# A preactivation block on Trainium2: x tiles on partitions 16 to 63 and 64 to 111, the first two heads' 1x1 product on quarters of TensorE, static output tiles, and the last stores over three queues

## The chip, the cores and the metric

The kernel runs on one core of one Trainium2 chip. The metric is the device time in microseconds of one execution; before the change the median of 3 runs is 3560.19 us (3558.02 to 3560.29). A core has TensorE (PE; PEld is its weight load), VectorE (DVE), ScalarE (ACT), GpSimd (POOL) and SyncE (SP), which in this kernel only issues DMAs; ACT and POOL issue some as well.[...]

## The reference

The input x is 1 x 48 x 256 x 256 in float32. Two residual layers follow each other:

```python
x = x + _L0_conv_ref(_gn(x), w_qkv, w_dw, temperature, w_proj)
x = x + _L1_conv_ref(_gn(x), Ws, Hs, Cs, 64)
# _gn: groupnorm with 16 groups of 3 channels, without scale or shift
# _L0_conv_ref:
qkv = jnp.einsum('bchw,oc->bohw', x, w_qkv)      # 1x1, 48 -> 144
qkv = dwconv3x3(qkv, w_dw)                       # depthwise
q, k, v = (heads(t) for t in jnp.split(qkv, 3, axis=1))   # 4x4 patches, padding 4, 8 heads
attn = softmax(einsum('bhcn,bhcm->bhnm', l2norm(q), l2norm(k)) * temperature)
out = fold(einsum('bhcn,bhnm->bhcm', v, attn))
out = jnp.einsum('bchw,oc->bohw', out, w_proj)
# _L1_conv_ref: sum over t of 3 terms, on windows of 64 x 64
out = jnp.einsum('bcphqw,twW,thH,tcC->bCpHqW', xb, Ws, Hs, Cs)
```

## The kernel before

The work goes through stages, here with their times in the trace from the start of the span.

Stage A (0 to 73 us): x is loaded into `xr`, a tile of 96 partitions x 128 rows x 256 columns: the upper half of the image on partitions 0 to 47 by the SP queue, the lower half on 48 to 95 by ACT's (L432). It comes in ten parts of 16, 16, 16, 16, 16, 16, 16, 8, 4 and 4 rows, and DVE runs `bn_stats` (L436) on every two rows as they come. POOL issues 35 small DMAs with the weights (L104, L108, L114). `group_stats` (L131 to L149) makes mean and rstd by small products on PE (pm, pv), `wq` (the first two heads' weights, both halves in one block diagonal of 96 x 72) and `wr` (the other six heads') are scaled with rstd (L439, L440), and products pb (L445) give the biases. Small products pk and pr (L479, one per head) prepare normalising constants; they have PSUM tiles of their own and run at 12 to 21 us.

Stage B (72 to 138): `pointwise` (L153) makes q, k and v of the first two heads. Each of its 64 products takes two rows of both halves, contracts over 96 partitions and gives 72 rows of 512 (L155; the profile lists two matmul records per product). ACT (L161) and DVE (L159) empty PSUM in turn, with the bias, into one of four rotating tiles `ot0` with 8 rows of each half. Two DMAs per tile, of 36 partitions with 8256 bytes each, go out on SP to the scratch tensor `t1` in DRAM (L493).

Stage C (138 to 287): the depthwise convolution of the first head (`depthwise_first`) reads the padded rows back from `t1` (pad), multiplies with diagonal matrices (diag) on PE, and stores qkv.

Attention (287 to 3163): for each head and block, PE multiplies keys by queries (L351), ACT takes the exponential (L588), PE multiplies with the values (L622, on quarter columns of 32), DVE adds the blocks (L636). The 1x1 product of the other six heads runs in strips (`Strip`) between these, its loads in `xs` at partitions 0 to 47 and 64 to 111, and so do the depthwise convolutions of the next head, at places that the loops write out by hand. In the last head the x tiles `xts` of the first three rounds of the next stage are loaded. `store` (L645) writes a pair of finished blocks of the last head's output to `os_` in DRAM, four DMAs a pair, all on POOL.

Stage E (3165 to 3301), the projection, in eight rounds of 16 rows of each half: SP loads `pot` (two DMAs of 48 partitions, 768 KB each, L798) and from round 3 on the x rows `pxt` (two more, L800); PE multiplies with `wp` (96 x 96, L812); DVE adds the product to x (L819) and takes `bn_stats` (L823); POOL stores the sum to `x1s` in DRAM (L828). Then SP loads windows of it as `lxq` (L785), to partitions 0 to 47 and 64 to 111, and a chain of small operations makes the second layer's statistics (L852 to L875).

The second layer (3308 to 3546) runs three products per window (L941, L965, L984) with evictions, and stores the output.

[...]a scheduler places the instructions, except in blocks whose order is written out (`manual_schedule`).

Of the kernel before, what the change touches and what calls it, by code (L numbers as in the profile page):

```python
# [17 lines left out]
C = 48  # L18
H = W = 256
HALF = H // 2  # L20
P2 = 2 * C
KS = 4
# [25 lines left out]
def conv_preact_kernel(  # L48
# [37 lines left out]
    ones = const.tile([C, 128], F32, name="ones")  # L86
# [3 lines left out]
    gm = const.tile([P2, P2], F32, name="gm")  # L90
    nc.gpsimd.dma_start(out=gm, in_=gmat)

    wq = const.tile([P2, 2 * M0], F32, name="wq")
    nc.vector.memset(wq, 0.0)
    wr = const.tile([64 + C, M1], F32, name="wr")
    wp = const.tile([P2, P2], F32, name="wp")
    nc.vector.memset(wp, 0.0)
    for s in range(2):  # L100
        r = slice(s * C, (s + 1) * C)
        for h in range(NH if s == 0 else H0):
            o = s * M0 + h * HC if h < H0 else (h - H0) * HC
            nc.gpsimd.dma_start(  # L104
                out=(wq[r] if h < H0 else wr[0:C])[:, o : o + HC].rearrange("c (z e) -> c z e", z=3),
                in_=w_qkvT.rearrange("c (z h e) -> h c z e", z=3, h=NH)[h],
            )
        nc.gpsimd.dma_start(out=wp[r, r], in_=w_projT)  # L108
# [9 lines left out]
    mean0 = const.tile([P2, 1], F32, name="mean0")  # L118
    rstd0 = const.tile([P2, 1], F32, name="rstd0")
    mean1 = const.tile([P2, 1], F32, name="mean1")  # L120
    rstd1 = const.tile([P2, 1], F32, name="rstd1")
# [8 lines left out]
    def group_stats(st, mean, rstd, pool, pspool, behind=lambda: None):  # L130

        mv = pool.tile([P2, 2], F32, name="mv")
        nc.vector.bn_aggr(mv, st.rearrange("p n s -> p (n s)"))
        pm = pspool.tile([P2, 1], F32, name="pm", tag="pstat")
# [3 lines left out]
        d = pool.tile([P2, 1], F32, name="gsd")  # L138
        nc.vector.tensor_sub(d, mv[:, 0:1], mean)
        e = pool.tile([P2, 1], F32, name="gse")  # L140
        nc.vector.scalar_tensor_tensor(e, d, d, mv[:, 1:2], ALU.mult, ALU.add)
        pv = pspool.tile([P2, 1], F32, name="pv", tag="pstat")
        nc.tensor.matmul(pv, lhsT=gm, rhs=e, start=True, stop=True)
        behind()
        f = pool.tile([P2, 1], F32, name="gsf")
        nc.vector.tensor_scalar_add(f, pv, EPS)
        g = pool.tile([P2, 1], F32, name="gsg")
# [4 lines left out]

    def pointwise(ps, dst, xs, on_vector=False):  # L153

        nc.tensor.matmul(ps[: 2 * M0], lhsT=wq, rhs=xs.rearrange("p a b -> p (a b)"), start=True, stop=True)  # L155
        src = ps[: 2 * M0].rearrange("p (a b) -> p a b", a=2)
        dst = dst[:, :, 1 : W + 1]
        if on_vector:
            nc.vector.tensor_scalar_add(dst, src, bias[: 2 * M0, 0:1])  # L159
        else:  # L160
            nc.scalar.activation(dst, src, AF.Identity, bias=bias[: 2 * M0, 0:1])  # L161
# [5 lines left out]
    class Strip:  # L167
# [5 lines left out]
        def load(self):  # L173
            self.xs = cv.tile([64 + C, SR, W], F32, name="xs", bufs=2)
            for s, rows in enumerate(both_halves(xc, SR * self.j, SR)):
                nc.sync.dma_start(out=self.xs[s * 64 : s * 64 + C], in_=rows)

        def run(self, pool):
            self.ot = ots[self.j % len(ots)]
            for i in range(0, SR, 2):  # L180
                ps = pool.tile([128, 2, 512], F32, name="big")
                for s in range(2):
                    r = slice(s * 64, s * 64 + C)
                    nc.tensor.matmul(  # L184
                        ps[:M1, s, :],
                        lhsT=wr[r],
                        rhs=self.xs[r, i : i + 2, :].rearrange("p a b -> p (a b)"),
                        start=True,
                        stop=True,
                    )  # L190
# [226 lines left out]
    with tc.tile_pool(name="xn", bufs=1) as xnp, tc.tile_pool(name="cst", bufs=1) as cst, tc.tile_pool(  # L417
        name="nps", bufs=2, space=PSUM
    ) as nps, tc.tile_pool(name="pw", bufs=4, space=PSUM) as pw:
# [5 lines left out]
        xr = xnp.tile([P2, HALF, W], F32, name="xr")  # L425
        parts = [16] * 7 + [8, 4, 4]
        st0 = cst.tile([P2, HALF * W // 512, 6], F32, name="st0")
        for i, LR in enumerate(parts):
            j = sum(parts[:i])
            for s in range(2):  # L430
                eng = nc.sync if s == 0 else nc.scalar
                eng.dma_start(  # L432
                    out=xr[s * C : (s + 1) * C, j : j + LR, :], in_=xc[:, s * HALF + j : s * HALF + j + LR, :]
                )
# [3 lines left out]

        nc.vector.tensor_scalar_mul(wq, wq, rstd0)  # L439
        nc.vector.tensor_scalar_mul(wr[0:C], wr[0:C], rstd0[0:C])  # L440
        nc.gpsimd.dma_start(out=wr[64 : 64 + C], in_=wr[0:C])
        for g, (w, k) in enumerate(((wq, P2), (wr, C))):
            m = w.shape[1]
            pb = nps.tile([128, 1], F32, name="pb0", tag="pstat")
            nc.tensor.matmul(pb[:m], lhsT=w[:k], rhs=mean0[:k], start=True, stop=True)  # L445
            nc.vector.tensor_scalar_mul(bias[:m, g : g + 1], pb[:m], -1.0)


# [16 lines left out]
        pk = nps.tile([NP1, NP1], F32, name="pk", bufs=1)  # L465
# [11 lines left out]
        pr = nps.tile([NP1, NH + 1], F32, name="pr", bufs=1)  # L477
        for i in range(NH + 1):
            nc.tensor.matmul(pr[:, i : i + 1], lhsT=row[:, i, :], rhs=ones[0:1, 0:1], start=True, stop=True)  # L479
# [4 lines left out]
        OR = 8  # L484
        for y in range(0, HALF, OR):
            ot = xnp.tile([2 * M0, OR, W + 2], F32, name="ot0", bufs=4)
            nc.gpsimd.memset(ot[:, :, 0:1], 0.0)
            nc.gpsimd.memset(ot[:, :, W + 1 : W + 2], 0.0)
            for i in range(0, OR, 2):
                ps = pw.tile([128, 512], F32, name="pw")  # L490
                pointwise(ps, ot[:, i : i + 2, :], xr[:, y + i : y + i + 2, :], on_vector=(i // 2 % 2 == 1))
            for s, rows in enumerate(both_halves(t1[0], y, OR, base=1)):
                nc.sync.dma_start(out=rows, in_=ot[s * M0 : (s + 1) * M0])  # L493
# [581 lines left out]
```

## Time and profile before

| | us |
|---|---|
| median of 3 runs | 3560.19 (3558.02 to 3560.29) |
| the profiled execution | 3547.51 |
| its span | 3545.7, at a granted clock of 0.979 |
| end of the statistics in stage A (last `bn_stats`) | 67.95 |
| first store of stage B issued, last one landed | 81.14, 137.9 |
| first depthwise product | 147.07 |
| last addition of attention | 3162.75 |
| first issue of pot, first product with it | 3165.48, 3178.16 |
| end of the projection's additions | 3300.76 |
| first product of the second layer | 3307.8 |

A line of the profile's groups gives the source line, the engine, the operation, the tiles written and read with partitions and elements, the count, then the busy time, the mean of one in ns, and the idle time of the engine just before with what ended it. A row of the stretches gives start and end, the length, the busy time of each engine in it, the granted clock of TensorE, the share of the DMA engines that was busy, and GB/s. A row of the timeline gives start, length and the instructions that follow each other. Busy matmuls can lie beside each other, so mean times count can be above the busy time.

### The profile page before, as it was taken

What the parts mean: (1) busy time and instruction counts of PE and PEld (TensorE: products, weight loads), DVE (VectorE), ACT (ScalarE), POOL (GpSimd) and SP (SyncE); (2) the same over time, 40 slices, a digit from 0 to 9 for tenths busy, and PEclk for the clock granted to TensorE, in tenths of its full rate; (3) what the DMA queues carried; (4) which work ended last, traced back from release to release, by engine and by line L of the source; (5) the groups of instructions that cost most, each with busy time, mean ns of one, the idle gap of its engine ahead of it and who ended that gap; (6) DMA issues with size and microseconds to landing.
All of it is one profiled execution on the core that took longest, in us unless ns stands there. A gap on an engine that the chain in (4) does not pass through costs nothing. (4 is left out here: it accounts for less than half of the span.)

```text
span 3545.7 us, 63152 instructions
## 1 busy us (share of the span) xinstructions
PE 3339.1 (94%) x25836; PEld 1859.1 (52%) x25836; DVE 1990.7 (56%) x2983; ACT 1900.0 (54%) x2890; POOL 562.6 (16%) x648
## 2 busy tenths in 40 slices
PE   2878999999999999999999999999999999985898
PEld 1334455555555555555555555555555555531576
DVE  5463675168726872687268727862786222238543
ACT  0245677557645664666467646764676444420343
POOL 2030112012201220122012211221122100000123
PEclk9998999999999999999999999999999999997999
DMA  7455666633332333333233323332333221039764
GB/s 161 165 116 155 164 171 170 178 108 93 83 84 84 95 90 79 86 96 92 78 87 95 88 79 86 96 88 78 85 94 93 75 54 37 19 73 281 204 168 108
DMA packets 229730, 384.13 MB, mean 108 GB/s; under 512 B 77058, under 2 KB 174706, under 8 KB 224920
## 3 DMA queue, kind: packets, MB, share of 16 engines
q1 hardware_dynamic: 191158, 264.95, 27.4%
q0 software_dynamic: 34784, 106.40, 13.3%
q10 hardware_dynamic: 3490, 8.64, 1.1%
q8 instruction: 207, 3.39, 0.4%
q14 instruction: 91, 0.75, 0.1%
HBM read 234.76 MB, written 144.90 MB: 107 GB/s over the span
## 5 line engine op out<-in xcount | busy, mean ns | idle before, releaser
L588 ACT ACTIVATE e<-big,nmx 128x1024 f32<-128x1024 f32 x1024 | 1144.7, 1118 | 907.0 <-PE big L351 889.1
L351 PE MATMUL big<-kt,qt 128*128 128x512 f32 x6144 | 1457.3, 394 | 31.2 <-DMA kt<-qkv 26.2
L622 PE MATMUL big<-e,vn 128*32 128x512 f32 x12288 | 1348.4, 593 | 1.0 <-DVE vn L606 1.0
L351 PEld LDWEIGHTS big<-kt,qt 128*128 128x128 f32 x6144 | 1141.3, 188 | 370.8 <-issue 121.1
L636 DVE TENSOR_TENSOR oacc<-big,oacc 128x1024 f32<-128x1024 f32 x359 | 438.3, 1221 | 760.8 <-PE big L622 760.8
L622 PEld LDWEIGHTS big<-e,vn 128*32 128x32 f32 x12288 | 384.5, 110 | 881.9 <-issue 815.8
L239 DVE SCALAR_TENSOR_TENSOR acc<-pad,dwt,acc 126x1024 f32<-126x1024 f32 x592 | 765.6, 1293 | 33.8 <-ACT acc L220 18.1
L309 POOL DMA_DIRECT2D qkv<-o x72 | 53.0, 737 | 1331.9 <-ACT o L293 1331.9
L303 POOL TENSOR_TENSOR ol<-o,oh 126x1024 fp32r<-126x1024 f32 x78 | 185.3, 2376 | 271.6 <-DVE ss L254 198.6
L602 DVE TENSOR_REDUCE zt<-zs 128x1 f32<-128x5 f32 x256 | 38.7, 151 | 327.1 <-ACT e L588 291.3
L588 ACT ACTIVATION_READ_ACCUMULATOR e<-big,nmx 128x1 f32 x1024 | 196.0, 191 | 0.0
L293 ACT COPY o<-acc 126x1024 f32<-126x1024 f32 x74 | 161.6, 2184 | 0.0
L812 PE MATMUL pps<-pot,wp 96*96 96x512 f32 x128 | 77.0, 765 | 58.7 <-DMA pot<-os__70 46.0
L972 ACT COPY lyt<-pb 128x1024 f32<-128x1024 f32 x69 | 69.9, 1012 | 111.0 <-PE pb L965 108.4
L191 ACT ACTIVATE ot<-big,bias 108x1024 f32<-108x1024 f32 x64 | 68.1, 1112 | 105.8 <-PE big L184 68.5
L220 ACT ACTIVATE acc<-pad,dwt 126x1024 f32<-126x1024 f32 x74 | 84.0, 1135 | 75.9 <-DMA pad<-t 67.8
L148 ACT ACT_TABLE_LOAD x2 | 2.6, 1283 | 204.5 <-DMA x1s<-pxt 153.2
L250 ACT ACTIVATE sq<-acc 126x1024 f32<-126x1024 f32 x74 | 78.4, 1059 | 60.0 <-DVE acc L239 49.1
L228 PE MATMUL dps<-pad,diag 126*126 126x512 f32 x216 | 96.0, 604 | 15.4 <-DMA pad<-t 15.4
L325 POOL DMA_DIRECT2D kt<-qkv x44 | 23.0, 543 | 516.5 <-PE big L351 504.3
L951 DVE COPY lzt<-pa 128x864 f32<-128x864 f32 (+1 forms) x69 | 67.4, 1000 | 59.7 <-PE pa L941 59.7
L254 DVE TENSOR_REDUCE ss<-sq 126x64 f32<-126x1024 f32 x80 | 97.3, 1218 | 6.2 <-ACT sq L250 6.2
(142 smaller groups left out, 1964.5 us busy)
## 6 DMA issues: line engine op xcount, KB each, us to landing
pad<-t SPq DMA_DIRECT2D x238, 254.0 KB
t<-ot SPq DMA_DIRECT2D x64, 435.4 KB
qkv<-ol POOLq DMA_DIRECT2D x78, 336.0 KB, 6.5
qkv<-oh POOLq DMA_DIRECT2D x70, 336.0 KB, 5.7
qt<-qkv SPq DMA_DIRECT2D x176, 96.0 KB
xs<-in_x_dram SPq DMA_DIRECT2D x64, 192.0 KB
pot<-os__70 SPq DMA_DIRECT2D x16, 768.0 KB
out_dram<-lrt POOLq DMA_DIRECT2D x96, 128.0 KB, 3.8
```

The costliest lines, as they stand in the source:

```text
L220: nc.scalar.mul(self.acc, self.pad[:, 0:KS, 0:W], dwt[:, self.h, 0:1])
L228: nc.tensor.matmul(ps[:, i, :], lhsT=diag[:, tap, :], rhs=self.pad[:, y : y + 2, dx : dx + W], start=(tap == 0), stop=(tap == 8),)
L239: nc.vector.scalar_tensor_tensor(self.acc, self.pad[:, dy : dy + KS, dx : dx + W], dwt[:, self.h, tap : tap + 1], self.acc, ALU.mult, ALU.add,
L250: nc.scalar.activation(self.sq, self.acc, AF.Square)
L254: nc.vector.tensor_reduce(self.ss, self.sq.rearrange("p a (x b) -> p x a b", b=KS), AX.XY, ALU.add)
L293: nc.scalar.copy(self.o.rearrange("p (a b) x -> p a b x", a=KS), self.acc.rearrange("p a (x b) -> p a b x", b=KS))
L303: eng.tensor_sub(self.ol, self.o, self.oh.bitcast(F32))
L351: nc.tensor.matmul(ps[:, i, :], lhsT=qt[:, r, q0 : q0 + 128], rhs=kts[2 * j + i][:, r // 2, :], start=(r == 0), stop=(r == 2),)
L588: nc.scalar.activation(e[:, j * 1024 : (j + 1) * 1024], ps.rearrange("p a b -> p (a b)"), AF.Exp, bias=nmx[:, b : b + 1], accum_out=zs[:, ...
L622: nc.tensor.matmul(ps[p * 32 : (p + 1) * 32, u, :], lhsT=vn[:, c * 32 : (c + 1) * 32], rhs=e[:, n * 512 : (n + 1) * 512], start=(i == 0), ...
L636: nc.vector.tensor_add(oaccs[h, pair], ps, old)
L812: nc.tensor.matmul(ps[:, i : i + step, :], lhsT=wp, rhs=ot[:, ki * KS + i : ki * KS + i + step, part * n : (part + 1) * n], start=True, st ...
```

## The change

The x tiles get 112 partitions in place of 96: the two halves lie on 16 to 63 and 64 to 111 (`OFF`, `PF`, `rows_of`), and the first 16 partitions are cleared: of `xr`, `pots` and `pxt` by copies on ACT (`clear`), of `xss` and `xts` by memsets on POOL. All the loads of x in stage A go on SP. The first two heads' product now works on quarters: a 64 x 64 part of TensorE for each of two row halves and two column halves, four products of two rows in two PSUM banks, which one 128 x 1024 eviction empties; the output tiles are four static ones (`oi0` to `oi3`) of 4 rows of each of four parts of the image, and their stores go half on SP, half on POOL. `wr`'s and `wq`'s second copies are made by DMAs inside SBUF before scaling. The small products pk and pr share the PSUM tag of the other statistics. `os_` is laid out so that one DMA loads a pot of 96 partitions; it stands ahead of the x loads. The last head's stores take turns on SP, ACT and POOL. In the statistics of the second layer a product pd1 is added, and `gm2` is made earlier. The diff, cut to its core:

```diff
+OFF = 16
+PF = OFF + P2
+    none = const.tile([OFF, 1], F32, name="none")
+    nc.vector.memset(none, 0.0)
+    ones = const.tile([1, 1], F32, name="ones")
     nc.vector.memset(ones, 1.0)
+    rows_of = [slice(OFF + s * C, OFF + (s + 1) * C) for s in range(2)]
+    gm = const.tile([PF, PF], F32, name="gm")
+    nc.vector.memset(gm, 0.0)
+    nc.gpsimd.dma_start(out=gm[OFF:, OFF:], in_=gmat)
+    wq = const.tile([PF, 64], F32, name="wq")
     nc.vector.memset(wq, 0.0)
-    wr = const.tile([64 + C, M1], F32, name="wr")
-    wp = const.tile([P2, P2], F32, name="wp")
+    wr = const.tile([PF, M1], F32, name="wr")
+    nc.vector.memset(wr, 0.0)
+    wp = const.tile([PF, PF], F32, name="wp")
     nc.vector.memset(wp, 0.0)
-    for s in range(2):
-        r = slice(s * C, (s + 1) * C)
-        for h in range(NH if s == 0 else H0):
-            o = s * M0 + h * HC if h < H0 else (h - H0) * HC
-            nc.gpsimd.dma_start(
-                out=(wq[r] if h < H0 else wr[0:C])[:, o : o + HC].rearrange("c (z e) -> c z e", z=3),
-                in_=w_qkvT.rearrange("c (z h e) -> h c z e", z=3, h=NH)[h],
-            )
+    for h in range(NH):
+        o = h * HC if h < H0 else (h - H0) * HC
+        nc.gpsimd.dma_start(
+            out=(wq if h < H0 else wr)[rows_of[0], o : o + HC].rearrange("c (z e) -> c z e", z=3),
+            in_=w_qkvT.rearrange("c (z h e) -> h c z e", z=3, h=NH)[h],
+        )
+    for w in (wq, wr):
+        nc.gpsimd.dma_start(out=w[rows_of[1]], in_=w[rows_of[0]])
+    for r in rows_of:
         nc.gpsimd.dma_start(out=wp[r, r], in_=w_projT)
+    def clear(t):
+        _, a, b = t.shape
+        to = none.rearrange("p (u v) -> p u v", u=1).to_broadcast([OFF, a, b])
+        nc.scalar.copy(t[:OFF], to)
...
-            self.xs = cv.tile([64 + C, SR, W], F32, name="xs", bufs=2)
+            self.xs = xss[self.j % len(xss)]
             for s, rows in enumerate(both_halves(xc, SR * self.j, SR)):
-                nc.sync.dma_start(out=self.xs[s * 64 : s * 64 + C], in_=rows)
+                nc.sync.dma_start(out=self.xs[rows_of[s]], in_=rows)
...
-    ) as nps, tc.tile_pool(name="pw", bufs=4, space=PSUM) as pw:
+    ) as nps, tc.tile_pool(name="pw", bufs=3, space=PSUM) as pw:
...
-        xr = xnp.tile([P2, HALF, W], F32, name="xr")
+        xr = xnp.tile([PF, HALF, W], F32, name="xr")
         parts = [16] * 7 + [8, 4, 4]
-        st0 = cst.tile([P2, HALF * W // 512, 6], F32, name="st0")
+        st0 = cst.tile([PF, HALF * W // 512, 6], F32, name="st0")
         for i, LR in enumerate(parts):
             j = sum(parts[:i])
-            for s in range(2):
-                eng = nc.sync if s == 0 else nc.scalar
-                eng.dma_start(
-                    out=xr[s * C : (s + 1) * C, j : j + LR, :], in_=xc[:, s * HALF + j : s * HALF + j + LR, :]
-                )
+            clear(xr[:, j : j + LR, :])
+            for s, rows in enumerate(both_halves(xc, j, LR)):
+                nc.sync.dma_start(out=xr[rows_of[s], j : j + LR, :], in_=rows)
             for i in range(0, LR, 2):
                 nc.vector.bn_stats(st0[:, (j + i) // 2, :], xr[:, j + i : j + i + 2, :].rearrange("p a b -> p (a b)"))
         group_stats(st0, mean0, rstd0, cst, nps)
-        nc.vector.tensor_scalar_mul(wq, wq, rstd0)
-        nc.vector.tensor_scalar_mul(wr[0:C], wr[0:C], rstd0[0:C])
-        nc.gpsimd.dma_start(out=wr[64 : 64 + C], in_=wr[0:C])
-        for g, (w, k) in enumerate(((wq, P2), (wr, C))):
+        for g, w in enumerate((wq, wr)):
+            nc.vector.tensor_scalar_mul(w, w, rstd0)
             m = w.shape[1]
             pb = nps.tile([128, 1], F32, name="pb0", tag="pstat")
-            nc.tensor.matmul(pb[:m], lhsT=w[:k], rhs=mean0[:k], start=True, stop=True)
+            if g:
+                nc.tensor.matmul(pb[:m], lhsT=w[:64], rhs=mean0[:64], start=True, stop=True)
+            for o in (0, 64) if g == 0 else ():
+                nc.tensor.matmul(pb[o : o + m], lhsT=w[:64], rhs=mean0[:64], start=True, stop=True)
+            m = 128 if g == 0 else m
             nc.vector.tensor_scalar_mul(bias[:m, g : g + 1], pb[:m], -1.0)
...
-        pk = nps.tile([NP1, NP1], F32, name="pk", bufs=1)
+        pk = nps.tile([NP1, NP1], F32, name="pk", tag="pstat")
         nc.tensor.matmul(pk, lhsT=pick, rhs=pick, start=True, stop=True)
...
-        pr = nps.tile([NP1, NH + 1], F32, name="pr", bufs=1)
+        pr = nps.tile([NP1, NH + 1], F32, name="pr", tag="pstat")
         for i in range(NH + 1):
-            nc.tensor.matmul(pr[:, i : i + 1], lhsT=row[:, i, :], rhs=ones[0:1, 0:1], start=True, stop=True)
+            nc.tensor.matmul(pr[:, i : i + 1], lhsT=row[:, i, :], rhs=ones, start=True, stop=True)
...
-        OR = 8
-        for y in range(0, HALF, OR):
-            ot = xnp.tile([2 * M0, OR, W + 2], F32, name="ot0", bufs=4)
-            nc.gpsimd.memset(ot[:, :, 0:1], 0.0)
-            nc.gpsimd.memset(ot[:, :, W + 1 : W + 2], 0.0)
+        OR = 4
+        QR = HALF // 2
+        ois = [xnp.tile([128, 2, OR, W + 2], F32, name=f"oi{i}") for i in range(4)]
+        for t in ois:
+            nc.gpsimd.memset(t[:, :, :, 0:1], 0.0)
+            nc.gpsimd.memset(t[:, :, :, W + 1 : W + 2], 0.0)
+        for n in range(QR // OR):
+            ot = ois[n % len(ois)]
             for i in range(0, OR, 2):
-                ps = pw.tile([128, 512], F32, name="pw")
-                pointwise(ps, ot[:, i : i + 2, :], xr[:, y + i : y + i + 2, :], on_vector=(i // 2 % 2 == 1))
-            for s, rows in enumerate(both_halves(t1[0], y, OR, base=1)):
-                nc.sync.dma_start(out=rows, in_=ot[s * M0 : (s + 1) * M0])
+                ps = pw.tile([128, 2, 512], F32, name="pw")
+                for c in range(2):
+                    for s in range(2):
+                        r = slice(s * 64, min(PF, s * 64 + 64))
+                        y = c * QR + n * OR + i
+                        nc.tensor.matmul(
+                            ps[c * 64 : (c + 1) * 64, s, :],
+                            lhsT=wq[r],
+                            rhs=xr[r, y : y + 2, :].rearrange("p a b -> p (a b)"),
+                            start=True,
+                            stop=True,
+                        )
+                dst, src = ot[:, :, i : i + 2, 1 : W + 1], ps.rearrange("p s (a b) -> p s a b", a=2)
+                if i:
+                    nc.vector.tensor_scalar_add(dst, src, bias[:, 0:1])
+                else:
+                    nc.scalar.activation(dst, src, AF.Identity, bias=bias[:, 0:1])
+            for c in range(2):
+                for s, rows in enumerate(both_halves(t1[0], c * QR + n * OR, OR, base=1)):
+                    (nc.gpsimd if s else nc.sync).dma_start(out=rows, in_=ot[c * 64 : c * 64 + M0, s])
...
+    xss = [cv.tile([PF, SR, W], F32, name=f"xs{i}") for i in range(2)]
+    for t in xss:
+        nc.gpsimd.memset(t[:OFF], 0.0)
...
-                    rows = os_[n * T : (n + 1) * T, h * HD + c : h * HD + c + p1 - p0, :]
-                    nc.gpsimd.dma_start(
+                    n, v = n % (NM // 2), n // (NM // 2)
+                    rows = os_.rearrange("(t v) c n -> v t c n", v=2)[v]
+                    rows = rows[n * T : (n + 1) * T, h * HD + c : h * HD + c + p1 - p0, :]
+                    eng = (nc.sync, nc.scalar, nc.gpsimd)[(2 * pair + u) % 3] if h == NH - 1 else nc.gpsimd
+                    eng.dma_start(
                         out=rows.rearrange("t c n -> c t n"),
...
-                        xts = [pe.tile([P2, RP, W], F32, name=f"xt{t}") for t in range(NX)]
+                        xts = [pe.tile([PF, RP, W], F32, name=f"xt{t}") for t in range(NX)]
+                        for t in xts:
+                            nc.gpsimd.memset(t[:OFF], 0.0)
...
-                            for half in range(2):
-                                y0 = half * HALF + t * RP + y
-                                nc.sync.dma_start(
-                                    out=xts[t][half * C : (half + 1) * C, y : y + RP // 4, :],
-                                    in_=xc[:, y0 : y0 + RP // 4, :],
-                                )
+                            for half, src in enumerate(both_halves(xc, t * RP + y, RP // 4)):
+                                nc.sync.dma_start(out=xts[t][rows_of[half], y : y + RP // 4, :], in_=src)
...
-    with tc.tile_pool(name="pj", bufs=3) as pj, tc.tile_pool(name="pjs", bufs=1) as pjs, tc.tile_pool(
+    with tc.tile_pool(name="pj", bufs=1) as pj, tc.tile_pool(name="pjs", bufs=1) as pjs, tc.tile_pool(
         name="pps", bufs=3, space=PSUM
     ) as pps, tc.tile_pool(name="pp1", bufs=1, space=PSUM) as pp1:
-        st1 = pjs.tile([P2, HALF * W // 512, 6], F32, name="st1")
-        ov = os_.rearrange("t (c k) n -> t c k n", k=KK)
+        st1 = pjs.tile([PF, HALF * W // 512, 6], F32, name="st1")
+        ov = os_.rearrange("(t s) (c k) n -> t (s c) k n", s=2, k=KK)
+        pots = [pj.tile([PF, KK, NP], F32, name=f"pot{t}") for t in range(3)]
+        xus = xts + [pj.tile([PF, RP, W], F32, name=f"pxt{t}") for t in range(3)]
+        for t in pots + xus[NX:]:
+            clear(t)
+        gm2 = pjs.tile([PF, 64 + C], F32, name="gm2")
+        nc.vector.memset(gm2, 0.0)
+        for o in (0, 64):
+            nc.vector.tensor_copy(gm2[:, o : o + C], gm[:, rows_of[0]])
         for t in range(HALF // RP):
-            ot = pj.tile([P2, KK, NP], F32, name="pot")
-            xt = xts[t] if t < NX else pj.tile([P2, RP, W], F32, name="pxt")
-            for s in range(2):
-                r = slice(s * C, (s + 1) * C)
-                y0 = s * HALF + t * RP
-                nc.sync.dma_start(out=ot[r], in_=ov[s * (NT // 2 // TP) + t])
-                if t >= NX:
-                    nc.sync.dma_start(out=xt[r], in_=xc[:, y0 : y0 + RP, :])
+            ot = pots[t % 3]
+            xt = xus[t if t < NX else NX + (t - NX) % 3]
+            nc.sync.dma_start(out=ot[OFF:], in_=ov[t])
+            if t >= NX:
+                for s, rows in enumerate(both_halves(xc, t * RP, RP)):
+                    nc.sync.dma_start(out=xt[rows_of[s]], in_=rows)
...
-                for s in range(2):
-                    y0 = s * HALF + t * RP + ys.start
-                    nc.gpsimd.dma_start(out=x1s[:, y0 : y0 + R, :], in_=xt[s * C : (s + 1) * C, ys])
+                for s, rows in enumerate(both_halves(x1s, t * RP + ys.start, R)):
+                    nc.gpsimd.dma_start(out=rows, in_=xt[rows_of[s], ys])
...
-        at = pjs.tile([C, 64 + CK], F32, name="at")
+        at = pjs.tile([64 + C, 64 + CK], F32, name="at")
...
-        gm2 = pjs.tile([P2, 64 + CK], F32, name="gm2")
-        nc.vector.memset(gm2, 0.0)
-        for o in (0, 64):
-            nc.vector.tensor_copy(gm2[:, o : o + C], gm[:, 0:C])
...
-            pc1 = pp1.tile([64 + CK, 1], F32, name="pc1", tag="pstat")
+            pd1 = pp1.tile([64 + C, 1], F32, name="pd1", tag="pstat")
+            nc.tensor.matmul(pd1, lhsT=gm2, rhs=mv1[:, 0:1], start=True, stop=True)
+            mcol = pjs.tile([64 + C, 64 + CK], F32, name="mcol")
+            nc.vector.tensor_scalar_mul(mcol, at, pd1)
+            pc1 = pp1.tile([64 + C, 1], F32, name="pc1", tag="pstat")
             nc.tensor.matmul(pc1, lhsT=gm2, rhs=e1, start=True, stop=True)
             occupy(nmx)
-            rstd2 = pjs.tile([64 + CK, 1], F32, name="rstd2")
+            rstd2 = pjs.tile([64 + C, 1], F32, name="rstd2")
             nc.vector.tensor_scalar_add(rstd2, pc1, EPS)
             nc.scalar.activation(rstd2, rstd2, AF.Sqrt)
             nc.vector.reciprocal(rstd2, rstd2)
-            nc.vector.tensor_scalar_mul(csn[: 64 + CK], csn[: 64 + CK], rstd2)
-            mcol = pjs.tile([C, 64 + CK], F32, name="mcol")
-            nc.vector.tensor_scalar_mul(mcol, at, mean1[0:C])
+            nc.vector.tensor_scalar_mul(csn[: 64 + C], csn[: 64 + C], rstd2)
             pb1 = pp1.tile([64 + CK, T3 * C], F32, name="pb1")
-            nc.tensor.matmul(pb1, lhsT=mcol, rhs=csn[0:C], start=True, stop=True)
+            nc.tensor.matmul(pb1, lhsT=mcol[0:C], rhs=csn[0:C], start=True, stop=True)
             occupy(nmx)
             nc.vector.tensor_sub(csn[: 64 + CK], csn[: 64 + CK], pb1)
     early.close()
```

## The prediction

> **What bounds the kernel now.** I read the shares of busy time first, then each engine's busy time stretch by stretch, then the groups of instructions, and last the waits of the SP queue and the timeline of DVE. The page says that attention on TensorE is nearly everything:
>
> ```profile
> PE 3339.1 (94%) x25836; PEld 1859.1 (52%) x25836; DVE 1990.7 (56%) x2983; ACT 1900.0 (54%) x2890; POOL 562.6 (16%) x648
> ```
>
> The stretches say where TensorE is not the limit. Columns: start and end, length, busy time of the five engines, granted clock, share of the DMA engines, GB/s.
>
> ```profile
> 0.00:64.00 64.00, 4.77 (x20) 4.40 (x20) 38.51 (x83) 1.28 (x1) 15.23 (x32) 1.00 0.96 199
> 80.00:134.00 54.00, 51.70 (x121) 17.02 (x119) 23.16 (x31) 20.51 (x30) 1.80 (x24) 1.00 0.56 168
> 287.00:3163.00 2876.00, 2865.07 (x19068) 1589.87 (x19067) 1633.45 (x2556) 1737.19 (x2710) 422.47 (x401) 1.00 0.36 93
> 3172.00:3174.40 2.40, 0.00 (x0) 0.00 (x0) 0.00 (x0) 0.00 (x0) 0.00 (x0) 0.50 1.10 323
> 3176.80:3179.20 2.40, 1.04 (x2) 0.50 (x3) 0.00 (x0) 0.00 (x0) 0.00 (x0) 0.50 0.98 130
> 3219.80:3287.90 68.10, 36.72 (x57) 12.45 (x58) 49.86 (x50) 0.00 (x0) 4.02 (x8) 0.65 1.00 286
> 3291.00:3297.00 6.00, 3.78 (x7) 1.10 (x7) 6.00 (x8) 0.00 (x0) 1.00 (x2) 0.84 1.00 199
> ```
>
> Three stretches are touched. A (0 to 64) loads x, with the DMA engines full: load-bound. B (about 72 to 138) is the first two heads' 1x1 product, PE 51.70 of 54 us busy, DMA engines at 0.56: PE-bound. E (3165 to 3301) is the projection; from 3219.8 on, DVE is busy 49.86 of 68.10 us with DMA at 1.00: DMA-bound. The 2876 us of attention between them are PE-bound (2865 busy) and not touched inside, nor is the second layer after 3308 (PE busy 216.65 of 232 us). So the change is worth what A, B and E together gain or lose.
>
> In B the groups are these (line, engine, operation, tiles, count, then busy us, mean ns, idle time before and its releaser):
>
> ```profile
> L155 PE MATMUL pw<-xr,wq 96*72 96x512 f32 x128 | 58.6, 620 | 0.0
> L159 DVE TENSOR_SCALAR ot<-pw,bias 72x512 f32<-72x512 f32 x32 | 23.9, 747 | 33.2 <-PE pw L155 33.2
> L161 ACT ACTIVATE ot<-pw,bias 72x512 f32<-72x512 f32 x32 | 21.9, 684 | 37.7 <-PE pw L155 37.7
> ```
>
> Both evicting engines wait for PE, so PE is last there. In E the SP queue waits so (line, cause, us in total, times, longest):
>
> ```profile
> SPq L798 <- DMA os__70<-oacc: 55.2, 2, 51.0
> SPq L798 <- PE pps L812: 34.4, 4, 11.3
> SPq L800 <- DMA x1s<-pxt: 33.0, 2, 19.5
> ```
>
> And DVE's timeline shows the rounds (start, length, ..., idle before and releaser in brackets):
>
> ```profile
> 3207.26 3.83 DVE L819 TENSOR_TENSOR xt<-pps,xt 96x1024 f32<-96x1024 f32 x2
> ...
> 3219.81 7.70 DVE L819 TENSOR_TENSOR pxt<-pps,pxt 96x1024 f32<-96x1024 f32 x4
> 3234.65 7.64 DVE L819 TENSOR_TENSOR pxt<-pps,pxt 96x1024 f32<-96x1024 f32 x4 [2.40 <-DMA pxt<-in_x_dram]
> ```
>
> Without a wait one round takes DVE 12.5 us (3207.26 to 3219.81). From round 3 on they begin at 3219.81, 3234.65, 3251.58, 3269.79 and 3287.86, 17.0 us apart on average, with DVE idle for a load of x or of pot.
>
> [...]in the pot loads a slow stretch (130 GB/s) and a fast one (323) follow each other. [...]in this trace the attention's quarter-column products run side by side (L622 is listed at 593 ns x 12288, 7287 us, in 1348 us of busy time). [...]
>
> **A.** Loads: the 12.58 MB of x come on the SP queue alone, to the two new sets of partitions. In the trace the same two kinds of place meet in the lxq loads, which go to partitions 0 to 47 and 64 to 111[...] on SP alone: 199 GB/s at 3291 to 3297. A's own steady rate is 204 (one pair of 16-row parts, 1.573 MB, each 7.7 us by the starts of their bn_stats groups). At 199 it is 7.9 us, and over eight pairs +1.7 us. Low end 0. High end: if only one half moves at a time[...], near the 130 to 145 GB/s of the slow stretch, +19 us. I take +1.7. The ACT copies of zeros are ten, 32768 elements per partition in all; at the 1.06 us of a 1024-element copy (L250) some 34 us, under the 63 us of loads: nothing, and at most 34 if the loads were instantaneous. The weight DMAs on POOL stay as many; the two copies inside SBUF replace loads, with the last work on POOL ending at 69.3 and rstd at 72.2: nothing (a late one would hold the first product, at most 2 us).
>
> **B.** PE: 128 products on quarters are 256 records. L984, the second layer's 64*64 product, is 576 records in 69.9 us of busy time, 121 ns each side by side; 256 of them make 31 us in place of 58.6. Evictions: 32 of 128x1024, 16 on ACT at 1.11 us (L191) and 16 on DVE at 1.25 us (L239, L636): 18 and 20 us side by side, below PE. So neither is last any more; the stores are. They are the same 9.51 MB, in 64 DMAs of 36 partitions x 4128 B instead of 32 x 8256 B, half on SP, half on POOL (32 issues at 0.74 us by L309, 24 us of an idle engine: nothing). Before they ran at 168 to 174 GB/s because PE paced them, with DMA share 0.56 to 0.58; 2-us slices reach 219. Inside one store cycle of 3.44 us the packets show about 2.3 us at 206 to 226 GB/s and then a tail of 1 us on a few engines, so there is little room: I take 180. [...]
>
> Start of the stores: with one PSUM tag for the small statistics, the nine pr products stand on PE behind the first pw products and ahead of the rest, and pk too; before they ran in A, hidden (18 records from 12.2 to 16.1 us). Queued behind them are all later pw, their evictions and stores. First store at 81.14 + 3.8 = 84.9 us. Last landing: 84.9 + 9510/r + 3 (flight of the last four), against 137.9; so B costs 9510/r - 50: at 180 +2.8, at 225 -7.7, at 145 +15.6 us. Behind it the padded loads wait for the landing, and then the 9.1 us to the first depthwise product (147.07) stay; POOL's two new memsets (2 x 1.3 us) shift diag (5.3 us from 138.25) to 2.6 us later, still at its side: 0 to +1.5, I take 0.
>
> **E.** The last head's stores leave over three queues instead of POOL's, where each group of four takes 2.33 us, the last from 3164.21; pot's first issue at 3165.48 can come 1 us earlier: -1 (0 to -2). A pot is now one DMA of 96 partitions[...]. Rounds 3 to 7 load 3.146 MB each; four steps took 68.1 us, 185 GB/s. At the 199 of the lxq loads four steps take 63.2: -4.9. Bounds: 0, and DVE's own 4 x 12.5 = 50, -18. The new order on SP (pot ahead of x) frees pot 6 from the wait on x1s, and puts pot 7 behind x of round 6: nothing by itself, up to +5 where that wait is long (19.5 us at worst). The six ACT clears (some 26 us) end before pxt is needed and cost the first pot only if it lands within 4 us. The ACT table load of 1.28 us (at 3304.39, after the last additions) waits for several DMAs before and for none in the new order, so it leaves the path; less 0.6 for the extra small product and scaling: -0.7. Sum of E: -1 - 4.9 - 0.7 = -6.6 (range -16 to +5).
>
> **Sum.** +1.7 + 2.8 - 6.6 = -2.1 us. The profiled execution took 3547.51 us (span 3545.7, 1.8 around it), so it would take 3545.4; the median of the runs is 3560.19, 12.7 above the profiled one, and the same -2.1 gives 3558. About 0.2%, 7 us, is what a measurement of this kernel can tell from no change.
>
> **The rivals.** Forecast: PE's halving is hidden by the stores, and E pays for A and B; own range 3547 to 3568. Rival F, stores near the bound: at 225 GB/s B gains 7.7, the sum is 1.7 - 7.7 - 6.6 = -12.6, 3547.6; with E at its better end 3540. For it: slices of 219 GB/s. Against: no stretch of 5 us above 182. It decides from 199 GB/s on. Rival S, on the other side: the stores of both queues collide, because at any time both carry the same 36-row sets. For it: the 1-us tails in the trace. Against: [...]four DMAs are there to mix. At 145 GB/s +15.6, sum +10.7: 3571; with x serialised in A, up to 3590. It decides below 154 GB/s. Rival N: the quarters don't run side by side, so 256 records at 430 ns make 110 us instead of 55, end about 53 us later: 3611; L984 in this kernel speaks against it.
>
> **How the numbers follow.** Forecast 0.45, F 0.22, S 0.28, N 0.05. Of the forecast's 0.45, 0.10 lie below 3553, 0.28 within 0.2%, 0.07 above 3567. Faster 0.10 + 0.22 = 0.32; same 0.28; slower 0.07 + 0.28 + 0.05 = 0.40. The range 3538 to 3588 leaves out N and the ends of F and S.
>
> **What would show it.** A: last bn_stats at 69.7 (67.95 before). B: the first store near 84.9, PE busy about 31 us with waits on ACT and DVE, those on stores; the last landing near 141 and the stretch at 180 GB/s. E: round starts 15.8 us apart. The forecast falls if the store rate in B leaves 154 to 199 GB/s, if A's pairs are over 8.5 us apart, or if the rounds in E stay at 17 us.

## The result, and the profile after

The changed kernel takes 3572.34 us (median of 7 runs, 3568.46 to 3576.26); the kernel before, over 7 runs, 3560.19 (3554.03 to 3568.7). The ratio is 1.0034, with a 95% interval of 1.0023 to 1.0045: about 12 us slower. The forecast was 3558, 2 us faster. The time lies in the range of 3538 to 3588, but on the other side.

The stretches of the changed kernel (same columns as before: start and end, length, busy time of PE, PEld, DVE, ACT and POOL, clock, DMA share, GB/s):

```profile
0.00:64.00 64.00, 0.00 (x0) 0.00 (x0) 27.73 (x64) 30.89 (x12) 15.64 (x33) 1.00 1.00 145
64.00:89.00 25.00, 0.00 (x0) 0.00 (x0) 14.21 (x24) 0.00 (x0) 7.67 (x22) 1.00 0.96 150
108.30:159.10 50.80, 31.40 (x228) 9.14 (x224) 19.25 (x15) 16.44 (x15) 16.09 (x32) 0.83 0.61 188
3246.90:3308.90 62.00, 39.23 (x58) 13.63 (x58) 49.74 (x50) 0.00 (x0) 4.02 (x8) 0.72 1.00 280
```

Stage A moves 145 GB/s where it moved 199, with the DMA engines as busy as before (share 1.00, 0.96 before), and it lasts to 89.4 us. Stage B's stores run at 188 (before 168, paced by PE), and in the projection DVE is busy 49.74 of 62 us (before 49.86 of 68.10). DVE's timeline shows the loads' pace:

```profile
15.50 4.83 DVE L436 BATCH_NORM_STATS2 st<-xr 112x6 f32<-112x512 f32 x8
25.88 4.85 DVE L436 BATCH_NORM_STATS2 st<-xr 112x6 f32<-112x512 f32 x8 [5.55 <-DMA xr<-in_x_dram]
36.94 4.85 DVE L436 BATCH_NORM_STATS2 st<-xr 112x6 f32<-112x512 f32 x8 [6.21 <-DMA xr<-in_x_dram]
47.60 4.84 DVE L436 BATCH_NORM_STATS2 st<-xr 112x6 f32<-112x512 f32 x8 [5.81 <-DMA xr<-in_x_dram]
```

A pair of 16-row parts comes every 10.9 us (25.88 to 69.38 in four steps), not every 7.7, and ahead of each group DVE waits over 5 us for the load. The groups of stage B:

```profile
L497 PE MATMUL pw<-xr,wq 64*64 64x512 f32 (+1 forms) x256 | 40.4, 725 | 9.7 <-ACT oi L508 9.7
L506 DVE TENSOR_SCALAR oi<-pw,bias 128x1024 f32<-128x1024 f32 x16 | 20.5, 1283 | 27.5 <-DMA t<-oi 15.6 <-PE pw L497 11.9
L508 ACT ACTIVATE oi<-pw,bias 128x1024 f32<-128x1024 f32 x16 | 17.7, 1115 | 40.2 <-PE pw L497 20.7 <-DMA t<-oi 19.6
```

PE now waits for the evictions (9.7 us), and these wait for the stores to free the static tiles (15.6 and 19.6 us): the chain that the forecast described. The quarters do run side by side, 256 records in 40.4 us at 725 ns each.

With the events that both traces share, the two profiled spans (3545.7 and 3574.5) fall into these pieces, in us:

```
                                            before    after   difference
start to the last bn_stats                    67.9     89.4     +21.4
to the first store                            13.2     19.0      +5.7
to the landing of the last store              56.8     50.8      -6.0
to the first depthwise product                 9.1      9.1       0.0
to the first product of attention            124.0    124.3      +0.4
to the last addition of attention           2892.9   2901.6      +8.7
to bn_aggr of the second layer               136.9    127.6      -9.3
to the first product of the second layer       7.0      9.0      +2.0
to the end                                   237.9    243.8      +5.9
```

The pieces that the change rewrites, the first three and the projection with the passage behind it, come to +13.8 us; the medians differ by 12.2. Nearly all of the rest, +14.6, lies in attention and in the second layer. The profiled executions are no typical pair: before's is 12.7 us under its median, after's 3.9 over its own. How far those two pieces scatter is seen below.

### The profile page after: what moved, and what is told of

Read it like the earlier page. It is cut to its first block, busy times and chain, and to the rows that moved or that the text cites. A ratio compares the mean times of both kernels' runs of the same rounds, so it can differ in the third digit from the quotient of the medians.

```text
span 3574.5 us, 63450 instructions
## 1 busy us (share of the span) xinstructions
PE 3335.5 (93%) x25968; PEld 1861.4 (52%) x25968; DVE 1991.2 (56%) x2970; ACT 1946.6 (54%) x2891; POOL 583.2 (16%) x652
## 4 chain that ended last, share of the span: by engine, by line
PE 83%; DMA 4%; DVE 2%; issue 1%; SPq 1%; ACT 0%; POOL 0%; POOLq 0%; DVEq 0%; ACTq 0%
PE big L353 39%; PE big L643 36%; PE pb L990 2%; PE pa L966 2%; PE pc L1009 2%; DMA xs<-in_x_dram 2%; PE big L186 1%; DMA pxt<-in_x_dram 1%; DVE acc L241 1%; PE pst L591 1%; DMA t<-ot 1%; DMA x1s<-pxt 1%; DVE xt L847 0%; SPq L327 0%; DVE st L851 0%
## 5 line engine op out<-in xcount | busy, mean ns | idle before, releaser
L840 PE MATMUL pps<-pot,wp 112*112 112x512 f32 x128 | 80.8, 797 | 45.0 <-DVE pxt L847 19.5
L990 PE MATMUL pb<-wsb,lzt 64*64 64x64 f32 x4608 | 89.5, 221 | 7.6 <-issue 4.9
```

The lines of the kernel that those rows point to most:

```text
L840: nc.tensor.matmul(ps[:, i : i + step, :], lhsT=wp, rhs=ot[:, ki * KS + i : ki * KS + i + step, part * n : (part + 1) * n], start=True, st ...
L990: nc.tensor.matmul(pb[s * WS : (s + 1) * WS, w, n * WS : (n + 1) * WS], lhsT=zts[u][r, t * C + b * 24 + q * 8 + s * 4 + i, :], rhs=wsb[r, ...
```

## The experiments

The main theory (P): in stage A the layout and the single queue act together. Each half of x, on its set of partitions, loads slowly when it loads alone (the guess was the 145 GB/s of the changed kernel), and one queue moves one half at a time, so that the two never load together. Rivals: the layout is slow by itself; one queue is too slow by itself; the copies of zeros slow the loads. A second question was what pays in B and E.

**Two queues.** In the changed kernel:

```diff
-            clear(xr[:, j : j + LR, :])
             for s, rows in enumerate(both_halves(xc, j, LR)):
-                nc.sync.dma_start(out=xr[rows_of[s], j : j + LR, :], in_=rows)
+                (nc.scalar if s else nc.sync).dma_start(out=xr[rows_of[s], j : j + LR, :], in_=rows)
+            clear(xr[:, j : j + LR, :])
```

> Changed kernel with one edit: the second half of x in stage A goes out on ACT's DMA queue, ahead of the copy of zeros of the same part; the first half stays on SP. Theory P ([...]one queue moves one half at a time, so that 145 GB/s is one half's limit): both halves move together, pairs of 16-row parts come 7.7 us apart or less, the last bn_stats ends at 64 to 69 us in place of 89.4, and the median falls by about 20 us against the changed kernel, to 3552, some 8 us below the kernel before. Rival L (the layout itself is slow, in any order): pairs stay above 10 us apart and the time stays at 3572. Rival Z (the copies of zeros on ACT or the weights on POOL slow the loads): the same, no gain.

Measured: 3561.06 us, ratio to the kernel before 1.0004 (0.9991 to 1.0017), so about 11 us of the loss are gone. As long as both queues had loads in flight the pairs came every 7.5 us (bn_stats at 21.23, 29.05, 36.23, 43.85), 209 GB/s: the new places are not slow by themselves, and the copies of zeros were there too. The last bn_stats came only at 75.2, later than expected. ACT's own timeline says why:

```profile
21.13 0.32 ACTq L433 DMA_DIRECT2D xr<-in_x_dram  x1
21.49 3.60 ACT L119 COPY xr<-none 16x4096 f32<-16x4096 f32 x1 [4.87 <-DMA xr<-in_x_dram]
43.01 0.32 ACTq L433 DMA_DIRECT2D xr<-in_x_dram  x1
43.36 3.60 ACT L119 COPY xr<-none 16x4096 f32<-16x4096 f32 x1 [18.27 <-DMA xr<-in_x_dram]
```

Its sixth load was issued at 43.01, after a wait for another load of x (ACT stood idle for 18.27 us before the next copy); SP had by then issued all its ten (the last at 36.2). The DMA view of this run (packets, MB, time as a share of 16 engines; q1 is SP's queue, q10 ACT's), first from 14 to 40 us, then from 42 to 50, shows what that did:

```profile
DMA packets 648, 5.53 MB, mean 213 GB/s; under 512 B 312, under 2 KB 312, under 8 KB 312
q10 hardware_dynamic: 223, 2.83, 50.4%
q1 hardware_dynamic: 213, 2.67, 49.2%
```

```profile
DMA packets 170, 1.11 MB, mean 139 GB/s; under 512 B 69, under 2 KB 103, under 8 KB 103
q1 hardware_dynamic: 85, 1.09, 90.5%
```

With both halves in flight the same places take 213 GB/s; while ACT's queue moves nothing and SP's half goes alone, 139. That fits the time, which missed the expected 3552 by 9 us.

**The kernel before on one queue.** `eng = nc.sync if s == 0 else nc.scalar` becomes `eng = nc.sync`.

> Kernel before with one edit: both halves of x in stage A on the SP queue, at the old places 0 to 47 and 48 to 95. Theory P: the half on 0 to 47 goes at about 139 GB/s, the one on 48 to 95 at about 240 (as in the pot loads), a pair of parts in 8.7 us, the last bn_stats at about 75 us (67.95 before). Rival Q (one queue cannot feed the engines, whatever the places): pairs 10.8 us apart as in the changed kernel, the last bn_stats at about 89.

Measured: last bn_stats at 77.1 us; the pairs came 9.1 us apart (31.13 to 67.49 in four steps), 173 GB/s. The stretches show two rates in turn, as of two halves that move one after the other (windows chosen inside the slow and the fast phases):

```profile
40.00:43.00 3.00, 0.00 (x0) 0.00 (x0) 2.63 (x5) 0.00 (x0) 0.58 (x2) 1.00 0.99 143
44.50:47.00 2.50, 0.00 (x0) 0.00 (x0) 0.70 (x2) 0.00 (x0) 0.70 (x2) 1.00 1.03 230
48.00:52.00 4.00, 0.00 (x0) 0.00 (x0) 2.76 (x5) 0.00 (x0) 0.69 (x2) 1.00 1.03 158
53.00:56.00 3.00, 0.00 (x0) 0.00 (x0) 1.08 (x2) 0.00 (x0) 0.98 (x2) 1.00 1.11 236
```

This is the pattern that theory P named, about 139 and about 240 in turn. On one queue the old places end stage A 9 us later than on two; the new places on one queue end it 21 us later than the kernel before. So the queue is not the whole, against rival Q, and the places decide how much it costs. The single time, 3550.49, is not told apart from the kernel before.

**Smaller parts on one queue.** In the changed kernel `parts = [16] * 7 + [8, 4, 4]` becomes `parts = [8] * 16`.

> Changed kernel with one edit: x in stage A, still on SP alone, comes in sixteen parts of 8 rows (two DMAs of 393 KB each) in place of ten of up to 16 rows (786 KB). These are the size of the lxq loads from which the prediction took 199 GB/s. Theory P1 (the queue moves one DMA of one half after another; with smaller DMAs the engines get out of step[...]): a pair of 16 rows in 8.0 to 8.7 us, last bn_stats at 70 to 76. Rival P2 (size has nothing to do with it; each half has 145 GB/s whenever one queue alternates them): pairs stay at 10.8 us and the last bn_stats at 87 to 91.

Measured: the last bn_stats at 74.1 in place of 89.4.

```profile
25.51 2.47 DVE L436 BATCH_NORM_STATS2 st<-xr 112x6 f32<-112x512 f32 x4 [1.95 <-ACT xr L119]
29.61 2.47 DVE L436 BATCH_NORM_STATS2 st<-xr 112x6 f32<-112x512 f32 x4 [1.63 <-DMA xr<-in_x_dram]
33.96 2.47 DVE L436 BATCH_NORM_STATS2 st<-xr 112x6 f32<-112x512 f32 x4 [1.88 <-DMA xr<-in_x_dram]
38.26 2.47 DVE L436 BATCH_NORM_STATS2 st<-xr 112x6 f32<-112x512 f32 x4 [1.83 <-DMA xr<-in_x_dram]
```

Each group is now eight rows of both halves, and they come 4.2 us apart (21.09 to 71.64 in twelve steps), 8.4 us for sixteen rows, 187 GB/s on the same single queue and at the same places. The single time, 3554.34, is 14 us below the fastest of the changed kernel's seven. The size of the DMAs was the hidden condition of the 199 GB/s that the prediction carried over. Two things shrink together here, the DMA (786 to 393 KB) and its packets (16 to 8 KB), as they do in the lxq loads; no run holds them apart, and why smaller DMAs mix better (P1's engines out of step) is argued, not shown.

**The small products ahead of the statistics.** In the changed kernel the code from `tabs` to `nmul3`, with pk and pr, is moved ahead of `group_stats`.

> Changed kernel with one edit: the small products pk and pr and what they need stand ahead of the statistics of stage A, so that they run during the loads. Expected if they cost what the prediction's step says: from the end of bn_stats to the first store 15 us in place of 18.9 (13.2 in the kernel before), stage A as in the changed kernel (end near 89.4). If another thing delays the first store[...]: 18 or more, as before the edit.

Measured: 12.5 us from the last bn_stats to the first store in place of 19.0; stage A as in the changed kernel (90.8). PE's timeline of the changed kernel shows what was removed; the run of 16 pw products stands behind pr on PE and begins at 103.17, as the 3.99 us of pr end:

```profile
96.64 0.78 PE L465 MATMUL pk<-pick 14*126 14x126 f32 x2
97.35 1.97 PE L497 MATMUL pw<-xr,wq 48*64 48x512 f32 x2
99.25 3.99 PE L478 MATMUL pr<-ones,row 1*126 1x1 f32 x18
103.17 3.69 PE L497 MATMUL pw<-xr,wq 64*64 64x512 f32 x16
```

The 4 us of pr were priced; pk, and the pw products that stand alone between it and pr (1.97 us), were named but not added. By the diff it is the shared PSUM tag that put pk and pr here; no run gave back the tag alone.

**Both repairs together.**

> Changed kernel with both edits together: x in stage A on two queues, pk and pr ahead of the statistics. Expected: last bn_stats at 64 to 69 us, first store 15 us later, the last landing near 131 us (137.9 in the kernel before), and a median of about 3548, 12 us below the kernel before.

Measured: 3554.77 us, ratio 0.9991 (0.9978 to 1.0003). The first store was 12.5 us after the last bn_stats (15 expected), but that came at 83.0: ACT's sixth load was issued at 49.99 us, later still. The expected time was missed for the reason seen in the first experiment.

**Balanced loads.** Both repairs, and the zeros written so that they hold up neither queue:

```diff
+        for i in range(4):
+            load_x(i)
+        for i, (j, LR) in enumerate(spans):
+            nc.vector.memset(xr[:OFF, j : j + LR, :], 0.0) if i < 3 else clear(xr[:, j : j + LR, :])
+        for i in range(4, len(parts)):
+            load_x(i)
```

> Changed kernel with both repairs of stage A, and the zeros of its tile written by DVE (three parts) and by ACT behind its first four loads, so that neither queue's loads run ahead of the other's. Theory P: pairs of parts 7.4 us apart to the end, last bn_stats at 66 us (75 and 83 with the two earlier edits, where ACT's sixth load was issued only at 43 and 50 us), first store 12.5 us later at 78, landing near 129, and a median of 3544 to 3549, faster than both kernels. If stage A does not get below 72 us, the two new sets of partitions themselves cost time.

Measured: 3547.9 us, ratio 0.9961 (0.9947 to 0.9975), faster than both kernels. Stage A:

```profile
0.00:64.00 64.00, 4.77 (x20) 4.40 (x20) 47.02 (x86) 19.16 (x9) 13.15 (x28) 1.00 0.99 194
```

194 GB/s, the last bn_stats at 69.7, not the 66 expected: SP had again issued all its loads by 36.8 us, ACT its last at 63.6. Against the changed kernel the ratios differ by 0.0073, 26 us (about 20 to 33 by the two intervals); the traces give 19.7 for stage A and 6.4 for the small products, 26.2. In the two later kernels with the same loads (strips_back, pe_shift) the last bn_stats came at 73.0 and 74.3, so stage A is worth 15 to 20 us. Either way the two steps cover the 12 us that the change lost.

**All stores of stage B on SP** (in two_queues, `nc.gpsimd if s else nc.sync` becomes `nc.sync`).

> As two_queues, but all stores of the first two heads on SP, none on POOL. The prediction took one rate for the stores, 180 GB/s. If the second queue is what raised it to 200 (9.51 MB from the first store at 94.12 to the landing at 141.6), stage B grows to 52 us or more from the first store to the landing in place of 47.4; if the quarters' tile and its partitions set the rate, it stays at 47 to 50.

Measured: 56.1 us from the first store to the landing in place of 47.4. The DMA view of these stretches, first stores_sp, then two_queues:

```profile
DMA packets 3084, 9.61 MB, mean 166 GB/s; under 512 B 768, under 2 KB 768, under 8 KB 3079
```

```profile
DMA packets 3588, 9.57 MB, mean 199 GB/s; under 512 B 1280, under 2 KB 1280, under 8 KB 3584
```

The same stores make 166 GB/s on one queue and 199 on two. By the packets of the two traces, eight or fewer were in flight at once for some 19 us of the stretch on one queue and for some 8 us on two, and more than twelve for hardly 2 us in either; the DMA view gives the engines' busy share as 55.0% with one queue and 30.1 + 32.5% with two. So the second queue fills gaps between stores. This is one run, but its 56.1 us lies above the 47.4 to 52.4 of all nine kernels that store over two queues; so the second queue is worth 4 to 9 us, and without it the quarters gain nothing over the 56.8 of the kernel before. A second queue without the quarters was not tried; there PE was busy for 51.70 of 54 us.

**Two DMAs per pot** (in two_queues).

```diff
-            nc.sync.dma_start(out=ot[OFF:], in_=ov[t])
+            for s in range(2):
+                nc.sync.dma_start(out=ot[rows_of[s]], in_=ov[t, s * C : (s + 1) * C])
```

> As two_queues, but each pot is loaded by two DMAs of 48 partitions, as in the kernel before. If the one DMA over both sets of partitions is where the projection's gain comes from, the time from the last addition of attention to bn_aggr goes back to 135 us or more (131.5 in two_queues, 136.9 in the kernel before); if the places of the tiles or the order of the loads bring the gain, it stays at 131.

Measured: 144.7 us from the last addition of attention to bn_aggr; two_queues has 131.5, the kernel before 136.9. PE's wait for pot, in pot_two and in two_queues (in all, times, longest):

```profile
PE pps L841 <- DMA pot<-os__70: 34.3, 6, 17.4
```

```profile
PE pps L840 <- DMA pot<-os__70: 18.3, 3, 13.7
```

The gain of the projection comes from the one DMA that covers both halves: the ten kernels that load a pot by one DMA take 125.5 to 131.5 us here. With two DMAs the new places are slower than the old ones (144.7 and 136.9 us), as in stage A on one queue (89.4 and 77.1). This is one run, and its total, 3582.0, holds also a long attention (2902.3) and a stage A of 78.4; it is read by this stretch only.

**The projection's part alone**, put into the kernel before.

> Kernel before with only the projection's part of the change: pot and x tiles on 16 to 63 and 64 to 111, one DMA per pot ahead of the x loads, the last head's stores over three queues, the small products of the second layer's statistics as changed. Stages A and B are those of the kernel before. Theory E1: the projection gains about 7 us (from the last addition of attention to bn_aggr 136.9 in the kernel before, 127.6 to 131.5 in the changed kernels so far) and the passage into the second layer and that layer itself lose what they gained (9 us in place of 7, and 241 to 246 in place of 238), so that the median stays at that of the kernel before, within 3 us. Rival E2: the loss in the second layer comes with stages A and B, and here the time falls by 7 us.

Measured: 3553.64 us, ratio 0.9992 (0.9981 to 1.0002); by its trace the projection takes 125.5 us (136.9 before), the passage 8.0 (7.0), the second layer 239.9 (237.9). The 11.4 us of the projection are in the trace, but the median shows only some 3 (7 less to 1 more by the interval), and that is not clear of no change. The profiled execution is the fastest of its 22. So neither expectation is met cleanly: more than E1's zero by the trace, less than E2's 7 by the median.

**The strips' x tiles at their old places**, in balanced_early: `xs` and a copy of the weights on partitions 0 to 47 and 64 to 111.

> As balanced_early, but the strips of the other six heads' product keep the places of the kernel before: their x tiles on partitions 0 to 47 and 64 to 111, with 48 rows of weights. In the profiles so far TensorE waited 3.5 to 5.9 us for these x loads in the three kernels with the old places, and 5.1 to 11.7 (mean 8.4) in the seven with the new; from the first product of attention to the last addition 2886.5 to 2892.9 against 2889.1 to 2902.3. Theory S1 (the new places make these loads late): the waits fall to 3.5 to 6 us, this stretch to about 2890 in place of 2897, and the median by 4 to 6 us below balanced_early, to 3543. Rival S2 (these waits scatter from run to run): no change of the median beyond 2 us.

Measured: 3548.3 us, ratio 0.9971 (0.9957 to 0.9984). TensorE's wait for these loads was 10.8 us, attention 2899.9: S1 has fallen. The waits scatter, 5.1 to 13.8 in the kernels with the changed stages A and B, wherever the tiles lie.

**A shifted instruction stream**, in balanced_early: `for _ in range(5):` ahead of the pr products.

> As balanced_early, with each of the nine pr products repeated five times, which adds 36 tiny products to TensorE's instruction stream while it is idle in stage A, and no work elsewhere. The second layer, whose program is the same in all kernels, took 237.7 to 239.9 us in the three kernels with the old stages A and B and 241.0 to 245.6 in the seven with the new; in its trace TensorE pauses at certain places of the stream for nothing that the profile names. Theory F (it matters where in the stream these places lie, and the change moved them): the pauses lie at other places, and the second layer takes a time different from 243 by 2 us or more, up or down. Rival G (the loss comes from what precedes the layer[...]): pauses and time stay as in balanced_early, 241 to 245.

Measured: 3546.49 us, ratio 0.9962 (0.9949 to 0.9975), the same as balanced_early. The second layer took 237.3 us in its trace (243.3 in balanced_early) and the unnamed pauses of TensorE lie at other places, 8 in place of 12: what theory F asked for. But the median did not follow (-1.4 us), so one profile is not enough, and F is not shown.

## Why the prediction was wrong, point by point

**A** is the step that failed. It took +1.7 us, "at 199 it is 7.9 us", from the lxq loads to partitions 0 to 47 and 64 to 111 on SP alone; measured were 10.9 us a pair and +21.4. The 199 GB/s came from 6 us of the trace, some 1.2 MB. The lxq loads are 393 KB each, the x loads 786 KB. At 393 KB the changed kernel makes 187 GB/s, at 786 KB 145. The prediction had the other end in its bounds (+19, "if only one half moves at a time"), and chose the wrong end because it compared places and queue and not the size of a DMA. Its +19 does not follow from its own figures either: at 145 GB/s a pair takes 10.85 us, 3.15 more than 7.7, and eight pairs give +25. The rates of the runs fit a single queue that moves one half at a time: 209 to 213 GB/s with both in flight, 139 with one alone and 145 when a single queue alternates them in large DMAs. Why a half alone is slow at its place was not shown.

**Rival S** put its collision in the stores of B and let x serialise in A as an extra. The sign was S's, but the place was A; that S's 3571 lies next to the measured 3572 is luck. B's stores went at 188 to 199 GB/s, far from the 154 below which S decides and at the 199 from which rival F does. Its point of decision for A, pairs over 8.5 us, was passed. The 225 GB/s of rival F were the author's estimate, 168 x 0.75 / 0.56, with 0.75 for 12 of 16 engines; in the trace before, from 90 to 130 us, exactly 12 packets of 8256 bytes were in flight for 45% of the time and more for 2.6%. The 145 GB/s of rival S were an estimate too.

**B.** The small products cost more than the 3.8 us forecast: the way to the first store grew by 5.7, and it shrank by 6.4 when they were moved away. PE took 40.4 us, not 31: still hidden, and evictions and stores were last as described. By the prediction's own formula the 50.8 us from the first store to the landing mean 199 GB/s, not 180. The two errors cancel: from the last bn_stats to the landing 69.8 us, 70.0 before, -0.2 against the forecast +2.8.

**E** was right by its stretches. Forecast -6.6, measured -9.3 + 2.0 = -7.3 in the two traces; the median of the projection's part alone, -3, neither confirms nor refutes it. The repaired kernel, 14 us below the kernel before, fits it better: by its trace 4.7 us are gained up to attention and 8.2 in the projection with the passage. The rounds came 15.5 us apart (forecast 15.8), here because one DMA fills both sets of places; the pot_two run shows that without it the x and pot loads would have lost time (144.7 us in place of 131.5), so the 199 GB/s were right here by that one DMA, which the prediction did not price. The table load of 1.28 us did leave the path (at 3216.69, before at 3304.39), but the passage grew by 2.0 in place of shrinking by 0.7. The small products that keep TensorE busy there took 1.17 us each; in the kernel before they took 0.65, and the granted clock was 0.50 from 3326 to 3330.7 (1.00 from 3302.7 to 3307.7, the same place before).

**What was held fixed** was not quite fixed: attention from 2886.5 to 2892.9 us in three profiles with the old stages A and B, from 2889.1 to 2902.3 in ten with the new; the second layer 237.7 to 239.9 and 237.3 to 245.6. Two explanations were tried, and neither was shown. That part stays open. The repaired kernel's gain over the changed one fits A and the small products alone, so the 12 us don't need it.

## What to carry to other kernels

Two halves of a tensor on two sets of partitions that load slowly alone (139 GB/s here) and faster together (213) paid when both were in flight at the same moment, by two queues (209 to 213) or by one DMA across both (the pots, 131.5 us for the projection in place of 144.7). Small alternating DMAs on one queue helped too (187 in place of 145). A transfer rate read from a trace belongs to its DMA size, its queue and its partitions together (the same x came at 145, 187 and 209 GB/s here); before it is carried to another step, compare all three. And a step that only changes a buffer tag can put hidden work in front of the first store (6.4 us here): read the order on the engine and price everything that is ahead of it.

## What was not expected of the hardware

The same 12.58 MB on one queue to the same partitions took 145 GB/s in DMAs of 786 KB and 187 in DMAs of 393 KB, with the DMA engines' busy share at about 1.00 in both. So a full share need not mean full speed: between 15 and 64 us a packet of 16 KB took 1.80 us (median) in the changed kernel and 1.21 in the kernel before, at shares of 1.01 and 0.97. The stores of 36 partitions made 166 GB/s from one queue and 199 from two, although hardly ever more than twelve of their packets were in flight at once in either.
